# A four-stage sequence model on one core: stages issued by virtual time, and the scan's decay computed in place

## The chip, the cores and the metric

The kernel runs on one core of one Trainium2 chip. The metric is the device time in microseconds of one launch, and the time of before is the median of three runs. Besides these there is one execution under the hardware profiler; every duration below comes from it.

## The reference

The input is sixteen sequences of 512 tokens with 256 features, float32. Each sequence passes through four residual blocks, each fed with a layernorm of its input:

```
x = x + mamba(layernorm(x))        # selective scan, 16 states for each of 256 features
x = x + ffn(layernorm(x))          # 256 -> 704 -> 256, silu gate
x = x + attention(layernorm(x))    # causal linear attention, 16 heads of 16, elu + 1
x = x + ffn(layernorm(x))          # the same weights again
```

Inside, cut to what matters:

```
# mamba: u = x w_in; dt, B, C are projections of u
dt = softplus(dt_low @ w_dt + b_dt) * (DT_MAX - DT_MIN) + DT_MIN
h[d, n] = exp(dt[d] * A[d, n]) * h[d, n] + sum over d of (dt * A * B * u)
y[d] = sum over n of (h[d, n] * C[n]) + Dp[d] * u[d]
# ffn: activations and weights are quantised to FP4 in blocks of 16 and back
h = silu(xq @ wq_gate) * (xq @ wq_up);  out = quant(h) @ wq_down
# attention: num / den, with running sums of k v and of k over time
```

The time step of the recurrence is the token, so one sequence's scan is a chain along 512 tokens. The term that is added to the state is the same for all 256 features.

## The kernel before, in words

**One sequence, four stages.** Tokens lie 128 to a partition group (four chunks), or features on partitions and tokens along the row. The program writes the stages as generators that yield now and then, and a driver decides which generator goes on next. The order in which instructions are written is a priority: the Tile framework then places each engine's instructions at build time, by readiness and that priority, and each engine runs its list in order.

**Scan.** `front(b)` computes layernorm statistics and turns x into features (`tT_m`). `prologue(b)` computes dt (lines 456 to 471, through the tile `soft`), writes dt to DRAM as `dd` in eight DMAs from SP's queue (L476), computes u (L467), C (`cm`), and the state's input term `inp` (L485 to L496). `mamba(b)` then makes 16 steps. In each, `spread` reads a slice of `dd` back, repeated over 16 partitions, into one of three tiles `sp` (L509); `decay` makes two exponentials (L521) and a square (L524) on ACT into one of `NBAR = 2` tiles `bar`; DVE runs the recurrence over 2 x 512 elements (L540) and multiplies with C (L544); PE sums over the states into `py` (L550). At the end of each half, ACT copies `py` to `yT` (L555), and after the second half the output is turned back and added to x (L377).

**FFN.** Quantise x (L230 to L252), two matmuls for gate and up in halves of 352 columns (L592), tanh on ACT (L598), two products on DVE (L599, L600), quantise h, transpose (L614), down projection (L627). The first FFN (`_f` in tile names) has buffers of its own, and so has the second (`_g`).

**Attention.** q and k features (L664 to L672), a copy `ko` of k with the even heads zeroed (L681), then for each chunk scores (L710), the causal mask on DVE (L717), values (L741), a denominator spread by POOL (`dx`, L751), and the projection (L788).

**Shared resources.** All PSUM results but `py` take turns in seven banks. The tags `soft` (used for `soft`, `dtu` and `yT`), `dt` (used for `dt` and `inp`), `u`, `cm` and `tT` have one buffer each, so `soft` of sequence b + 1 can only be written once `yT` of sequence b has been read.

**The driver.** For each b, `first(b)` is scan b with `front(b + 1)` woven in, followed by the first FFN of b with `prologue(b + 1)` woven in. `by_turns` shares out each part: the scan goes beside `last_ffn(b - 2)`, and the first FFN with the prologue goes beside `attention(b - 1)`. While scan 0 runs, the FFN weights are quantised and transposed beside it.

Of the kernel before, what the change touches and what calls it, by code (L numbers as in the profile page):

```python
# [17 lines left out]
P = 128  # L18
# [14 lines left out]
def kernel(  # L33
# [31 lines left out]
    NBAR = 2  # L65
    NSP = 3
# [20 lines left out]
    xp = ctx.enter_context(tc.tile_pool(name="xp", bufs=4))  # L87
# [10 lines left out]
    begun, turned, stats = {}, {}, {}  # L98
# [59 lines left out]
    for t in vpads:  # L158
        nc.gpsimd.memset(t, 0.0)

# [283 lines left out]
    def prologue(b):  # L444

        xnT = turned.pop(b)
# [18 lines left out]
        u = one.tile([P, ND, S], F32, tag="u", name=f"u_{b}")  # L465
        for e in range(ND):
            nc.scalar.copy(u[:, e, :], from_xn(w_in_sb[:, :, ts(e, P)], f"pu{e}"))  # L467
        yield 0.5
# [11 lines left out]
        cm = one.tile([P, S], F32, tag="cm", name=f"cm_{b}")  # L480
        nc.scalar.copy(cm, from_xn(w_c_sb, "pcm"))


        dtu = one.tile([P, ND, S], F32, tag="soft", name=f"dtu_{b}")
        nc.vector.tensor_tensor(dtu, dt, u, ALU.mult)  # L485
        pg = bank(f"pg_{b}")
        for k in range(ND):
            nc.tensor.matmul(
                pg, a_rep[:, k].rearrange("p n i -> p (n i)"), dtu[:, k, :],
                start=(k == 0), stop=(k == ND - 1),  # L490
            )
        pb = from_xn(w_b_sb, "pbm")
        inp = one.tile([P, 2, S], F32, tag="dt", name=f"inp_{b}")
        nc.scalar.copy(inp[:, 0, :], pb)
        nc.vector.tensor_tensor(inp[:, 1, :], inp[:, 0, :], pg, ALU.mult)
        nc.scalar.copy(inp[:, 0, :], inp[:, 1, :])  # L496
        begun[b] = (u, dd, inp, cm)
        yield 2.5

    def mamba(b, xt):  # L500
        u, dd, inp, cm = begun.pop(b)

        yT = one.tile([P, ND, S], F32, tag="soft", name=f"yT_{b}")

        def spread(e, j, q0):

            sp = one.tile([P, 2, S], F32, tag="sp", name=f"sp_{b}_{e}_{j}_{q0}", bufs=NSP)
            src = dd[e, q0 // 2, j * G8 : (j + 1) * G8].rearrange("i q t -> i (q t)")
            nc.sync.dma_start(  # L509
                sp.rearrange("p q t -> p (q t)"),  # L510
                src.unsqueeze(0).to_broadcast([NS, G8, 2 * S]),
            )
            return sp

        def decay(sp, e, j, q0):

            bar = bars[state["bar"] % NBAR]
            state["bar"] += 1
            for i in range(2):
                g = 16 * e + 4 * (q0 + i) + j  # L520
                nc.scalar.activation(  # L521
                    bar[:, i, 1:S], sp[:, i, 1:S], AF.Exp, scale=a_col[:, g : g + 1]
                )
# [4 lines left out]
        sps = [spread(*steps[at]) for at in range(NSP - 1)]  # L528
        ahead = decay(sps[0], *steps[0])
        for at, (e, j, q0) in enumerate(steps):  # L530
            bar = ahead
            if at + NSP - 1 < len(steps):
                sps.append(spread(*steps[at + NSP - 1]))
            if at + 1 < len(steps):
                ahead = decay(sps[at + 1], *steps[at + 1])
            if j == 0 and q0 == 0:
                py = ps_y.tile([P, S], F32, tag="y", name=f"py_{b}_{e}")
                nc.tensor.matmul(py, d_diag[:, e], u[:, e, :], start=True, stop=False)
            h = one.tile([P, 2, S], F32, tag="hs", name=f"h_{b}_{e}_{j}_{q0}", bufs=3)
# [14 lines left out]
            if j == 3 and q0 == 2:  # L554
                nc.scalar.copy(yT[:, e, :], py)  # L555
# [15 lines left out]
    def ffn(i, nm, b, xt):  # L571
# [77 lines left out]
    def attention(b, xt):  # L649
# [29 lines left out]

        ko = att.tile([P, ND, S], F32, tag="ko", name=f"ko_{b}", bufs=1)  # L680
        nc.scalar.activation(ko, kf, AF.Copy, scale=odd_heads[:, 0:1])  # L681
        yield 0.1

        def scores(c):
# [19 lines left out]

            psc = [bank(f"psc_{b}_{c}_{g}") for g in range(4)]
            for s in range(NH // 4):
                e, odd = divmod(s, 2)
                for g in range(4):
                    rows = slice(32 * g, 32 * g + (2 * HD if odd else HD))
                    nc.tensor.matmul(  # L710
                        psc[g][:, ts(s, P)], (ko if odd else kf)[rows, e, tok],
# [15 lines left out]
        def attend(c, vp, sm):  # L727
# [22 lines left out]
            dx = att.tile([P, ND * HB, HD], F32, tag="dx", name=f"dx_{b}_{c}")  # L750
# [11 lines left out]
            if c < NC - 1:  # L762
# [3 lines left out]
                kt = att.tile([P, D], F32, tag="kt", name=f"kt_{b}_{c}")  # L766
# [71 lines left out]
    def first(b, scanned=False):  # L838
# [3 lines left out]
        more = b + 1 < B  # L842
        fr = front(b + 1, xs[b + 1]) if more else iter(())
        if not scanned:
            yield from weave(mamba(b, xs[b]), fr, 6)
        yield from fr
        yield from weave(ffn(0, "f", b, xs[b]), prologue(b + 1) if more else iter(()), 0)

    def last_ffn(b, i=1):
        yield from ffn(i, "g", b, xs[b])  # L850
        nc.sync.dma_start(out[b].rearrange("(c p) d -> p c d", p=P), xs[b])

    FIRST, CHUNKS, FRONT, ATTN, FFN2 = 76.0, 30.0, 4.15, 23.0, 40.0

    def some(gen, total):

        done = 0.0
        while done < total:  # L860
            piece = next(gen, None)
            if piece is None:
                return
            done += piece
            yield piece

    def by_turns(halves):

        done = [0.0] * len(halves)
        alive = list(range(len(halves)))  # L870
        while alive:
            i = min(alive, key=lambda i: done[i] / halves[i][1])
            try:
                done[i] += next(halves[i][0])
            except StopIteration:
                alive.remove(i)
# [56 lines left out]
```

## Time and profile before

| | |
|---|---|
| median of three runs | 2849.86 us (2844.62 to 2854.19) |
| profiled execution, its time | 2856.84 us |
| profiled execution, its span | 2855.1 us |
| mean granted TensorE clock | 0.929 |
| first scan step starts | 57.2 us |
| last scan step starts | 2568.8 us |

The span runs from the first instruction of the program to the last. PE is TensorE's matmuls, PEld its weight loads, DVE is VectorE, ACT ScalarE, POOL GpSimd, SP the engine from whose queue nearly all DMAs are issued. "L540" is line 540 of the kernel. Busy time of an engine is the union of its instructions' durations. Matmuls overlap in the pipeline and their ends are modelled, so a PE that is shown as busy is not necessarily full. In a group of instructions, the last part of a line gives the engine's idle time just before them and what ended it.

### The profile page before, as it was taken

What the parts mean: (1) busy time and instruction counts of PE and PEld (TensorE: products, weight loads), DVE (VectorE), ACT (ScalarE), POOL (GpSimd) and SP (SyncE); (2) the same over time, 40 slices, a digit from 0 to 9 for tenths busy, and PEclk for the clock granted to TensorE, in tenths of its full rate; (3) what the DMA queues carried; (4) which work ended last, traced back from release to release, by engine and by line L of the source; (5) the groups of instructions that cost most, each with busy time, mean ns of one, the idle gap of its engine ahead of it and who ended that gap; (6) DMA issues with size and microseconds to landing.
All of it is one profiled execution on the core that took longest, in us unless ns stands there. A gap on an engine that the chain in (4) does not pass through costs nothing.

```text
span 2855.1 us, 34186 instructions
## 1 busy us (share of the span) xinstructions
PE 2450.1 (86%) x12907; PEld 1451.0 (51%) x12907; DVE 2433.6 (85%) x3545; ACT 1493.4 (52%) x2798; POOL 154.6 (5%) x153
## 2 busy tenths in 40 slices
PE   6577989898988889898898989989898888988997
PEld 3143555454554545455554545545455454545664
DVE  7797888989798898979888898888979889897565
ACT  4666455555545555554555555555554555553322
POOL 2000000000000000000000000000000000000000
PEclk7788999999999999999999999999899999999988
DMA  5332104132230313213031320403222041320000
GB/s 146 89 96 74 52 1 106 36 82 60 56 73 13 102 39 82 60 38 89 15 96 45 82 60 9 110 23 85 56 59 74 8 103 38 74 59 7 2 1 15
DMA packets 64376, 165.26 MB, mean 58 GB/s; under 512 B 8434, under 2 KB 26836, under 8 KB 64212
## 3 DMA queue, kind: packets, MB, share of 16 engines
q1 hardware_dynamic: 62592, 162.03, 22.0%
q8 instruction: 101, 1.65, 0.2%
q10 hardware_dynamic: 1620, 1.06, 0.1%
q14 instruction: 63, 0.52, 0.1%
HBM read 146.28 MB, written 16.78 MB: 57 GB/s over the span
## 4 chain that ended last, share of the span: by engine, by line
DVE 45%; PE 38%; ACT 8%; issue 6%; POOL 2%; DMA 0%; SPq 0%; ACTq 0%; DVEq 0%; POOLq 0%
DVE h L540 15%; PE po_g L627 5%; DVE h L544 5%; PE pg_g L592 4%; PE pu_g L592 4%; PE pqk L664 3%; DVE sm L717 3%; PE po_f L627 3%; PE pu_f L592 2%; PE pg_f L592 2%; DVE amax_f L230 2%; PE py L550 2%; DVE v_f L244 2%; DVE h_f L600 2%; DVE x L377 1%
## 5 line engine op out<-in xcount | busy, mean ns | idle before, releaser
L540 DVE TENSOR_TENSOR_SCAN h<-bar,inp 128x1024 f32<-128x1024 f32 x256 | 581.6, 2281 | 31.8 <-ACT inp L496 22.4
L521 ACT ACTIVATE bar<-sp,a_col 128x511 f32<-128x511 f32 x512 | 348.6, 715 | 287.6 <-DVE h L540 278.9
L550 PE MATMUL py<-h,red 128*32 128x512 f32 x1024 | 284.7, 712 | 111.6 <-DVE h L544 111.6
L544 DVE TENSOR_TENSOR h<-h,cm 128x1024 f32<-128x1024 f32 x256 | 310.7, 1214 | 1.0
L524 ACT ACTIVATE bar<-bar 128x1022 f32<-128x1022 f32 x256 | 269.8, 1054 | 5.6
L627 PE MATMUL po_f<-wdT,hqT_f 128*128 128x256 f32 (+1 forms) x768 | 205.8, 412 | 24.8 <-ACT hqT_f L618 24.8
L627 PE MATMUL po_g<-wdT,hqT_g 128*128 128x256 f32 (+1 forms) x768 | 200.1, 403 | 31.4 <-ACT hqT_g L618 31.4
L627 PEld LDWEIGHTS po_f<-wdT,hqT_f 128*128 128x128 f32 (+1 forms) x768 | 142.7, 199 | 120.3 <-ACT hqT_f L618 61.3
L592 PE MATMUL pg_f<-wgT,tT_f 128*128 128x352 f32 x512 | 191.3, 498 | 12.8 <-DVE sm L717 9.5
L592 PE MATMUL pu_f<-wuT,tT_f 128*128 128x352 f32 x512 | 178.5, 472 | 18.7 <-DVE sm L717 18.4
L627 PEld LDWEIGHTS po_g<-wdT,hqT_g 128*128 128x128 f32 (+1 forms) x768 | 138.6, 193 | 92.0 <-ACT hqT_g L618 45.2
L592 PE MATMUL pg_g<-wgT,tT_g 128*128 128x352 f32 x512 | 178.3, 471 | 0.0
L592 PE MATMUL pu_g<-wuT,tT_g 128*128 128x352 f32 x512 | 173.2, 460 | 0.0
L717 DVE TENSOR_TENSOR sm<-psc,causal 128x512 f32<-128x512 f32 x256 | 162.9, 676 | 5.4 <-PE psc L710 4.1
L248 ACT ACTIVATE big_f<-v_f 128x704 bf16<-128x704 f32 (+1 forms) x80 | 67.4, 842 | 166.9 <-DVE v_f L244 166.3
L592 PEld LDWEIGHTS pu_f<-wuT,tT_f 128*128 128x128 f32 x512 | 99.2, 196 | 80.9 <-DVE sm L717 25.7
L550 PEld LDWEIGHTS py<-h,red 128*32 128x32 f32 x1024 | 35.7, 116 | 203.6 <-DVE h L544 171.1
L592 PEld LDWEIGHTS pg_g<-wgT,tT_g 128*128 128x128 f32 x512 | 94.9, 191 | 73.4 <-issue 33.4
L592 PEld LDWEIGHTS pg_f<-wgT,tT_f 128*128 128x128 f32 x512 | 92.8, 197 | 76.1 <-issue 17.7
L592 PEld LDWEIGHTS pu_g<-wuT,tT_g 128*128 128x128 f32 x512 | 97.8, 191 | 54.7 <-issue 1.0
L664 PE MATMUL pqk<-tT_a,w_qkv_sb 128*128 128x512 f32 x256 | 125.1, 617 | 0.0
L598 ACT ACTIVATE h_g<-pg_g 128x352 f32<-128x352 f32 x128 | 59.0, 461 | 95.6 <-PE pg_g L592 94.8
(235 smaller groups left out, 4614.7 us busy)
## 6 DMA issues: line engine op xcount, KB each, us to landing
sp<-dd SPq DMA_DIRECT2D x256, 512.0 KB, 4.7
x<-in_L_attn_a_x_dram SPq DMA_DIRECT2D x16, 512.0 KB, 5.0
dd<-dt SPq DMA_DIRECT2D x128, 64.0 KB, 1.7
out_dram<-x SPq DMA_DIRECT2D x16, 512.0 KB, 4.5
w_qkv_sb<-in_L_attn_b_W_attn_dram ACTq DMA_DIRECT2D x1, 768.0 KB, 7.2
raw_d<-in_L_ffn_w_down_dram SPq DMA_DIRECT2D x1, 704.0 KB
raw_g<-in_L_ffn_w_gate_dram SPq DMA_DIRECT2D x1, 640.0 KB, 7.2
raw_u<-in_L_ffn_w_up_dram SPq DMA_DIRECT2D x1, 640.0 KB, 6.5
```

Source lines behind the costliest of these rows:

```text
L230: nc.vector.tensor_reduce(amax, src.rearrange("p (b k) -> p b k", k=BLK), AX.X, ALU.max, apply_absolute_value=True,)
L248: nc.scalar.activation(big, v, AF.Abs, scale=STEP)
L521: nc.scalar.activation(bar[:, i, 1:S], sp[:, i, 1:S], AF.Exp, scale=a_col[:, g : g + 1])
L524: nc.scalar.activation(bar[:, :, 1:S], bar[:, :, 1:S], AF.Square)
L540: nc.vector.tensor_tensor_scan(h.rearrange("p i t -> p (i t)"), bar.rearrange("p i t -> p (i t)"), inp.rearrange("p i t -> p (i t)"), 0.0, ...
L544: nc.vector.tensor_tensor(h, h, cm.unsqueeze(1).to_broadcast([P, 2, S]), ALU.mult)
L550: nc.tensor.matmul(py[32 * q : 32 * q + 32, :], red[:, j, :], (h0, h)[q // 2][:, q % 2, :], start=False, stop=(j == 3),)
L592: nc.tensor.matmul(pw[:, :HF], xqT[:, k, ts(c, P)], wT[:, k, cols], start=(k == 0), stop=(k == ND - 1),)
L598: nc.scalar.activation(hc, pg[:, :HF], AF.Tanh, scale=0.5)
L627: nc.tensor.matmul(po[:, :D], hqT[:rows, r, :], wdT[:rows, r, :], start=(r == 0), stop=(r == NR - 1),)
L664: nc.tensor.matmul(pz, w_qkv_sb[:, k, ts(je, P)], xnT[:, k, :], start=(k == 0), stop=(k == ND - 1),)
L717: nc.vector.tensor_tensor(t, psc[g].rearrange("p (s t) -> p s t", t=P), causal.unsqueeze(1).to_broadcast([P, NH // 4, P]), ALU.mult,)
```

## The change

It concerns the order of work, and the way in which the scan gets its decay.

- **The driver.** `first`, `some`, `by_turns` and the nested halves go. Each stage of each sequence gets a start and a length in virtual time, and `run_all` always lets the stage that is furthest behind go on. Scan b fills period b; the first FFN takes 0.9 of the next one, attention 0.8 of the one after (from b + 1.95), the second FFN 0.9 from b + 2.8. Four sequences are under way.
- **The prologue moves.** `front` is now the first part of `prologue`, and `prologue(b + 1)` is woven into scan b, not into the first FFN of b. It holds dt first, and C; then it waits (`halfway`) until scan b has started its second half, since u of scan b is read until then, and computes u and the input term.
- **Buffers for it.** `inp` gets its own tag, and its two equal halves are filled at the start of the scan from `term`, one by ACT and one by POOL. `dt * u` is written over dt. `yT` is allocated when the first half ends. `cm` gets two buffers, `xp` five.
- **Decay in place of dt.** `sp` goes. The DMA brings dt straight to `bar`, 511 elements for each of two rows and starting at the second element, and the exponentials run in place. `NBAR` goes from 2 to 4, and a step's slice is asked for three steps ahead.
- **Attention.** `ko` is made chunk by chunk (128 x 256 each) instead of at once; `dx` and `kt` have one buffer instead of two.

```diff
-    NBAR = 2
-    NSP = 3
+    NBAR = 4
...
-    xp = ctx.enter_context(tc.tile_pool(name="xp", bufs=4))
+    xp = ctx.enter_context(tc.tile_pool(name="xp", bufs=5))
...
-    def prologue(b):
+    def prologue(b, xt):
 
+        yield from front(b, xt)
         xnT = turned.pop(b)
...
-        cm = one.tile([P, S], F32, tag="cm", name=f"cm_{b}")
+        cm = one.tile([P, S], F32, tag="cm", name=f"cm_{b}", bufs=2)
         nc.scalar.copy(cm, from_xn(w_c_sb, "pcm"))
-        dtu = one.tile([P, ND, S], F32, tag="soft", name=f"dtu_{b}")
-        nc.vector.tensor_tensor(dtu, dt, u, ALU.mult)
+        yield 0.1
+        while halfway[0] < b:
+            yield 0
+        u = one.tile([P, ND, S], F32, tag="u", name=f"u_{b}")
+        for e in range(ND):
+            nc.scalar.copy(u[:, e, :], from_xn(w_in_sb[:, :, ts(e, P)], f"pu{e}"))
+        yield 0.5
+        nc.vector.tensor_tensor(dt, dt, u, ALU.mult)
...
-        pb = from_xn(w_b_sb, "pbm")
-        inp = one.tile([P, 2, S], F32, tag="dt", name=f"inp_{b}")
-        nc.scalar.copy(inp[:, 0, :], pb)
-        nc.vector.tensor_tensor(inp[:, 1, :], inp[:, 0, :], pg, ALU.mult)
-        nc.scalar.copy(inp[:, 0, :], inp[:, 1, :])
+        term = dt[:, 0, :]
+        nc.scalar.copy(term, from_xn(w_b_sb, "pbm"))
+        nc.vector.tensor_tensor(term, term, pg, ALU.mult)
...
+        inp = one.tile([P, 2, S], F32, tag="inp", name=f"inp_{b}")
+        nc.scalar.copy(inp[:, 0, :], term)
+        nc.gpsimd.tensor_copy(inp[:, 1, :], term)
 
         def spread(e, j, q0):
-            sp = one.tile([P, 2, S], F32, tag="sp", name=f"sp_{b}_{e}_{j}_{q0}", bufs=NSP)
-            src = dd[e, q0 // 2, j * G8 : (j + 1) * G8].rearrange("i q t -> i (q t)")
-            nc.sync.dma_start(
-                sp.rearrange("p q t -> p (q t)"),
-                src.unsqueeze(0).to_broadcast([NS, G8, 2 * S]),
-            )
-            return sp
-        def decay(sp, e, j, q0):
             bar = bars[state["bar"] % NBAR]
             state["bar"] += 1
+            src = dd[e, q0 // 2, j * G8 : (j + 1) * G8, :, 1:S]
+            nc.sync.dma_start(bar[:, :, 1:S], src.unsqueeze(0).to_broadcast([NS, G8, 2, S - 1]))
+            return bar
+
+        def decay(bar, e, j, q0):
...
-                    bar[:, i, 1:S], sp[:, i, 1:S], AF.Exp, scale=a_col[:, g : g + 1]
+                    bar[:, i, 1:S], bar[:, i, 1:S], AF.Exp, scale=a_col[:, g : g + 1]
...
-        sps = [spread(*steps[at]) for at in range(NSP - 1)]
+        sps = [spread(*steps[at]) for at in range(NBAR - 1)]
...
-            if at + NSP - 1 < len(steps):
-                sps.append(spread(*steps[at + NSP - 1]))
             if at + 1 < len(steps):
                 ahead = decay(sps[at + 1], *steps[at + 1])
+            if at + NBAR - 1 < len(steps):
+                sps.append(spread(*steps[at + NBAR - 1]))
...
+    def scan(b):
+        if b + 1 < B:
+            xs.append(load(b + 1))
+            yield from weave(mamba(b, xs[b]), prologue(b + 1, xs[b + 1]), 1)
+        else:
+            yield from mamba(b, xs[b])
...
+    SCAN, FFN, ATTN = 65.7, 40.2, 25.7
+
+    def run_all(stages):
+        under_way = []
+        while stages or under_way:
+            if not under_way or (stages and stages[0][0] <= min(u[0] for u in under_way)):
+                begin, length, total, stage, *args = stages.pop(0)
+                under_way.append([begin, length / total, stage(*args)])
+                continue
+            now = min(under_way, key=lambda u: u[0])
+            try:
+                now[0] += next(now[2]) * now[1]
+            except StopIteration:
+                under_way.remove(now)
...
+    for b in range(B):
+        if b > 0:
+            stages.append((b, 1.0, SCAN, scan, b))
+        stages.append((b + 1.0, 0.9, FFN, ffn, 0, "f", b, xs))
+        stages.append((b + 1.95, 0.8, ATTN, attention, b, xs))
+        stages.append((b + 2.8, 0.9, FFN, last_ffn, b))
+    run_all(sorted(stages, key=lambda stage: stage[0]))
```

## The prediction, made before the change was run

> **What bounds the kernel now.** I read the page's busy shares first, then the span cut at the scan's own starts and ends (the view of windows), then DVE in order of time inside one of those stretches.
>
> ```profile
> PE 2450.1 (86%) x12907; PEld 1451.0 (51%) x12907; DVE 2433.6 (85%) x3545; ACT 1493.4 (52%) x2798; POOL 154.6 (5%) x153
> ```
>
> PE and DVE seem to be about equally busy, and neither is full. That is an average over two regimes. One sequence's scan runs from 778.0 to 882.4, the next starts at 945.3; the columns are busy time with instruction counts for PE, PEld, DVE, ACT, POOL, then granted clock, DMA share, GB/s:
>
> ```profile
> core 0: us, PE busy (x) PEld busy (x) DVE busy (x) ACT busy (x) POOL busy (x), PEclk, DMA share, GB/s
> 778.00:882.40 104.40, 86.43 (x584) 51.46 (x583) 101.45 (x138) 58.07 (x109) 8.04 (x7) 0.95 0.28 71
> 882.40:945.30 62.90, 59.72 (x221) 35.77 (x220) 47.99 (x83) 34.24 (x66) 1.01 (x1) 1.00 0.17 42
> ...
> 0.00:57.20 57.20, 36.16 (x111) 21.36 (x111) 39.59 (x69) 23.70 (x41) 17.04 (x27) 0.85 0.48 139
> ...
> 2571.00:2855.00 284.00, 242.40 (x1355) 160.94 (x1353) 183.72 (x326) 80.26 (x186) 7.10 (x12) 0.91 0.02 6
> ```
>
> While a scan runs, DVE is 97% busy (101.45 of 104.4) and PE 83%. Between two scans, PE is 95% busy (59.72 of 62.9) and DVE only 76%. So the period of 167.3 us holds 149.44 us of DVE work and 146.15 us of PE work, and the two engines are the bound in turn. DVE's idle time is 2.95 + 14.91 = 17.9 us per period, nearly all of it between the scans.
>
> Why is no scan work there to fill it? DVE in order of time at the end of that stretch (start, duration, engine, line, tiles; in brackets the idle time before and what ended it):
>
> ```profile
> 929.56 1.21 DVE L471 SCALAR_TENSOR_TENSOR dt<-soft,dt 128x1024 f32<-128x1024 f32 x1
> ...
> 943.04 0.69 DVE L495 TENSOR_TENSOR inp<-inp,pg 128x512 f32<-128x512 f32 x1 [5.31 <-ACT inp L494]
> 945.29 2.29 DVE L540 TENSOR_TENSOR_SCAN h<-bar,inp 128x1024 f32<-128x1024 f32 x1 [1.57 <-ACT inp L496]
> ```
>
> The next scan waits for its own prologue, which ends 62 us after the previous scan did. The prologue can't begin before yT is read (tag `soft`), and it is woven into the first FFN, so it stands in PE's saturated queue. The stretch is a serial link between scan b and scan b + 1.
>
> The groups that carry the scan and the edited parts:
>
> ```profile
> L540 DVE TENSOR_TENSOR_SCAN h<-bar,inp 128x1024 f32<-128x1024 f32 x256 | 581.6, 2281 | 31.8 <-ACT inp L496 22.4
> L521 ACT ACTIVATE bar<-sp,a_col 128x511 f32<-128x511 f32 x512 | 348.6, 715 | 287.6 <-DVE h L540 278.9
> ...
> L544 DVE TENSOR_TENSOR h<-h,cm 128x1024 f32<-128x1024 f32 x256 | 310.7, 1214 | 1.0
> ...
> sp<-dd SPq DMA_DIRECT2D x256, 512.0 KB, 4.7
> ```
>
> **The change part by part.**
>
> *Prologue under the scan.* This is the part that matters. It removes the link: when scan b ends, only `inp` of b + 1 has to be filled (one ACT copy of 0.61 us, the L496 row's mean, and a POOL copy), so scan work is always there for DVE. Its instructions are the same and move from the PE-bound stretch to beside the scan: per sequence 16 matmuls for statistics and transposition (1.95 us in a row), 28 of 512 columns and 16 ACT passes, 5.4 us of DVE, one x load (5.0 us to landing) and eight `dd` writes (1.7 us each). The writes now stand in SP's queue among the spreads; each issue takes about 0.45 us (8 took 3.63 us at 930.8), so a spread is held 3.6 us, of the lead worked out below. Its own chain, from the load to `term`, took 52 us (from the pt_m matmuls at 891 to 943) beside a full PE, and the `halfway` wait takes it to the scan's second half at the latest: some 75 us of a 154 us scan remain after it. I cost it at nothing; uncovered, each 10 us of lateness would be 10 us per period.
>
> *Order by virtual time.* DVE's and PE's totals do not change. If all four streams are mixed evenly, a period needs 149.44 / 0.97 = 154.1 us of DVE and 146.15 / 0.95 = 153.8 us of PE, each at the best share that it shows today. Both would have to be near their best at once. I take DVE at 95% instead, 157.3 us, 10 us less than 167.3.
>
> How hard PE presses is where a rule matters. The Trainium skill, Perfetto Trace Analysis, Identifying the Most-Contended Engine, says that matmul busy time misjudges a PE's load and that weight-load busy time (or MFU) should be used. By the PE row, PE would be at 93% (146.15 of 157.3) and two nearly full in-order engines would block each other; I'd put DVE no higher than 91%, a period of 164. By the rule it is (51.46 + 35.77) / 157.3 = 55%, and DVE alone counts, at 97%: 154. The trace is between: in the PE-bound stretch weight loads stand at 57% (35.77 of 62.9) with PE clearly saturated, so 55% is not much room; but there the matmuls lay under 0.95 of busy time for at least 63 us on end. That is why I take 95%, and keep both ends.
>
> *Decay in place, four bars.* The page's largest ACT wait, 278.9 us for `bar` behind the scan's read, goes: an exponential now waits only for its DMA. What waits is the spread on SP's queue, for the scan step three earlier; behind it are other spreads, `dd` writes, x loads and outputs. The lead is three steps of about 157 / 16 = 9.8 us, 29 us, against 4.7 us to landing. ACT was not the bound (52%), and while it waited DVE was 97% busy: gain 0 to 3% of the scan stretch, inside my 95%. The price is in the DMA: rows of 511 elements (2044 B) instead of 1024 (4096 B). Perfetto Trace Analysis, DMA Optimizations, speaks against it: transfers under 2 KB have a significant overhead each. The row is 4.7 us for 512 KB; no row has this shape. If the landing doubled to 9.4 us it would still be under 29, and DMA engines that are 28% busy would be at most 56% busy. So 0 by both; if the lead were gone, 16 x 4.7 = 75 us per sequence would be exposed.
>
> *POOL's half of `inp`.* ACT loses nothing (two copies before, two after); POOL gains 16 copies of 128 x 512. `dx`, 128 x 256, takes 0.55 us on average, so 1.1 us each, at the scan's start. GPSIMD Engine Reference, Key points, says that POOL shares its SBUF interfaces with VectorE when that reads two SBUF inputs, as the scan does: at worst 16 x 1.1 = 18 us. In the trace the scan step has a median of 2282 ns and a maximum of 2380, though 64 `dx` copies and 64 `rstd` steps of 1.0 to 1.9 us run on POOL meanwhile, so I take 0 and keep 18.
>
> *The rest.* `ko` in chunks: 4 passes of about 0.37 us (the 128 x 256 copies, e.g. L767) for one of 1.15, so 0.33 us more ACT per sequence, hidden at 52%. One buffer for `dx` and `kt`: chunk c + 1's waits for chunk c's transposes; chunks are about 30 us apart (a fifth of a period and more), so 0; if not covered, under 1 us a chunk, 64 us at most. `cm`, `xp`: only more room.
>
> **The sum.** The head to the first scan stays 57.2. The tail has the same content (the trace has the 14th sequence's second FFN and the 15th's attention after the last scan already): 284, of which I take 280, since the last sequence's FFN no longer starts late. Between them lie 2433.6 - 39.6 - 183.7 = 2210.3 us of DVE work, which took 2514 us (88%). At 95% it takes 2327. Sum 2664, 191 less than the span of 2855.1. The profiled execution's time was 2856.8, 7 above the median of 2849.9; I give 2660 for the median.
>
> **The rivals.**
>
> *A: the mix reaches only 91%.* Both engines nearly full, matmul results waiting in seven banks for a DVE that is busy with 2.28 us scan steps. 2210.3 / 0.91 = 2429, with 337 for the ends 2766, some 2762. For it: the PE row as weighed above. Against: during a scan DVE keeps 97% with three other streams about.
>
> *B, slower: banks.* Scores take four of the seven banks at once (`psc`) until DVE has masked them (0.68 us each, L717), and FFN halves take two each. Today half of this is evacuated by a DVE with 24% idle; with four streams each DVE consumer stands behind scan steps for the whole period, PE stops for want of banks, and DVE then for want of PE. It decides from the point where DVE's share of the middle falls under 2210.3 / (2855 - 337) = 88%; at 83%, which is a period of 180, the time is 2663 + 337 = 3000. For it: PE waits of this kind (`pu_f` behind `sm`, 25.7 us in all) exist. Against: they are small in a scan stretch that has the same mixture.
>
> *C: it doesn't do what it says.* The framework orders instructions by readiness, and the trace has the stages of four sequences beside each other already. If the list comes out much the same and the link merely moves, the time stays at 2840 to 2858.
>
> *D: both engines are better than I take.* 97% and a tail of 250: 2279 + 307 = 2586.
>
> **How the numbers follow.** The likeliest, 2600 to 2720, has 0.60; A (2720 to 2840) 0.16; D 0.04; C 0.03; B 0.17. About 0.3%, 9 us, is what a measurement of this kernel can tell from no change. So faster 0.80, same 0.03, slower 0.17. The range leaves out B, and D's lower end, and holds the rest with POOL's 18 us: 2580 to 2850.
>
> **What would show it right or wrong.** Right: scan starts some 157 us apart with no stretch between the last step of one and the first of the next; DVE at 93% or more in every period; the ACT wait for `bar` behind L540 gone; `inp` no longer waited for by several us; half-clock stretches fewer, clock above 0.93. Wrong: weight loads waiting for `sm` or `x` by hundreds of us (B), `bar` waiting for the spread's DMA or SP's queue, scan steps longer than 2.3 us beside POOL, the first step late after `term`, or a tail much above 284 us.

## The result and the profile after

The changed kernel takes 3004.32 us (median of four runs, 3003.07 to 3005.55) against 2847.6 for before (median of four, one run more than in the table above): a ratio of 1.0547, 95% interval [1.0526, 1.0568]. It is slower by 157 us where 190 less were forecast, and lies outside the range. The profiled execution has a span of 3001.4 us and a granted clock of 0.885 (before 0.929).

The busy shares on the page of after, to be held against the same line of before:

```profile
PE 2484.2 (83%) x12907; PEld 1528.3 (51%) x12907; DVE 2452.6 (82%) x3545; ACT 1485.8 (50%) x2846; POOL 184.9 (6%) x171
```

The instructions are the same in number on PE and DVE, and DVE's work has grown by 19 us only. What grew is idle time: DVE's from 421 to 549 us of the span, PE's from 405 to 517. The span of after cut into its head, one period between two first scan steps (1070 to 1248) with two stretches inside it, and the end from the last scan step on (columns as in the windows of before):

```profile
core 0: us, PE busy (x) PEld busy (x) DVE busy (x) ACT busy (x) POOL busy (x), PEclk, DMA share, GB/s
0.00:61.00 61.00, 33.90 (x103) 19.74 (x103) 43.47 (x90) 29.55 (x50) 18.71 (x31) 0.83 0.52 147
1070.00:1158.00 88.00, 69.01 (x305) 43.41 (x302) 78.45 (x113) 52.66 (x101) 8.23 (x5) 0.83 0.31 78
1158.00:1236.00 78.00, 70.96 (x436) 43.87 (x435) 60.00 (x96) 34.68 (x67) 1.48 (x3) 0.96 0.11 28
1070.00:1248.00 178.00, 151.45 (x801) 94.03 (x797) 150.41 (x219) 91.75 (x177) 10.91 (x9) 0.89 0.22 56
2636.00:3001.40 365.40, 298.05 (x1665) 201.89 (x1662) 221.95 (x396) 100.89 (x243) 9.64 (x15) 0.89 0.02 6
```

The scan does start directly after the scan. But the period is 178.0 us where before's was 167.3, and it holds the same work: DVE 150.41 us (84.5%), PE 151.45 (85%). The two regimes of before haven't gone: they have moved inside the period. In its first 88 us DVE is 89% busy (78.45) and PE 78%; in the next 78 us PE is 91% busy (70.96) and DVE 77%. The end is 365.4 us long and holds 221.95 us of DVE work, 38 more than the last 284 us of before.

What the first regime looks like, in DVE's order of time in that period:

```profile
1086.41 0.88 DVE L230 TENSOR_REDUCE amax_f<-h_f 128x44 f32<-128x704 f32 x1
...
1088.28 1.16 DVE L230 TENSOR_REDUCE amax_g<-xn_g 128x64 f32<-128x1024 f32 x1
...
1092.59 1.21 DVE L244 TENSOR_TENSOR v_g<-xn_g,inv_g 128x1024 f32<-128x1024 f32 x1
1093.72 0.88 DVE L251 SCALAR_TENSOR_TENSOR v_f<-big_f,v_f 128x704 f32<-128x704 bf16 x1
1094.52 0.16 DVE L389 TENSOR_SCALAR var_m<-mv_m 128x4 f32<-128x4 f32 x1
1094.59 2.28 DVE L541 TENSOR_TENSOR_SCAN h<-bar,inp 128x1024 f32<-128x1024 f32 x1
1096.79 0.86 DVE L252 TENSOR_TENSOR h_f<-v_f,half_f 128x704 f32<-128x704 f32 x1
```

Three stages want DVE together: the first FFN quantises h (`h_f`), the second FFN quantises its input (`xn_g`), and the scan runs. PE in the same stretch, and what it waits for (brackets):

```profile
1086.42 4.57 PE L631 MATMUL po_f<-wdT,hqT_f 128*128 128x256 f32 x12 [2.53 <-ACT hqT_f L622]
1090.92 1.98 PE L551 MATMUL py<-h,red 128*32 128x512 f32 x12
1097.71 1.36 PE L618 MATMUL pt_h_f<-ident,h_f 128*128 128x128 f32 x6 [4.81 <-DVE h_f L252]
```

PE's next instruction needs `h_f`, whose last pass stands behind the scan step and the other FFN's passes; PE is idle for 4.81 us. From 1158 on it is the other way round: PE has matmuls of both FFNs in a row, and DVE is short of work. Over the whole execution, the list of waits has for PE's weight loads, first before, then after:

```profile
PEld pt_h_f L614 <- DVE h_f L252: 7.2, 2, 3.6
```

```profile
PEld pt_h_f L618 <- DVE h_f L252: 93.3, 16, 7.3
```

A wait that came twice comes about once in every sequence. Kernels without it will turn out to be as slow, though. And the decay: two groups of after and its two largest ACT waits.

```profile
L541 DVE TENSOR_TENSOR_SCAN h<-bar,inp 128x1024 f32<-128x1024 f32 x256 | 578.5, 2277 | 24.0 <-PE py L551 13.7 <-ACT bar L523 6.4 <-POOL inp L506 2.6
bar<-dd SPq DMA_DIRECT2D x256, 511.0 KB, 4.7
```

```profile
ACT bar L520 <- DMA bar<-dd: 261.3, 141, 9.1
ACT h_g L602 <- PE pg_g L596: 212.8, 84, 11.8
```

The wait behind the scan's read (278.9 us) is gone and one of the same size for the DMA stands in its place. The other line, tanh waiting for the gate's matmuls, was 94.8 us in before. The scan step itself costs what it did (2277 ns, 2281 before), and it waits little for `bar` (6.4 us in all): what pays is what stands behind the exponential in ACT's list. The chain that ended last shows it, at the start of the same stretch (start, us, engine, tile):

```profile
1075.92 6.23 DMA bar<-dd
...
1082.80 0.71 ACT bar L520
...
1084.35 0.94 ACT bar L523
...
1085.90 0.48 ACT hqT_f L622
...
1086.42 4.58 PE po_f L631 x12
```

The copy `hqT_f`, on which the down projection waits, stands in ACT's list behind exponentials that wait for the DMA. Over the whole execution `bar<-dd` is 8% of this chain; in before DMA is 0% of it.

### The profile page after: what moved, and what is told of

Same layout as the page of the kernel before. It is cut to its first block, busy times and chain, and to the rows that moved or that the text cites. A ratio compares the mean times of both kernels' runs of the same rounds, so it can differ in the third digit from the quotient of the medians.

```text
span 3001.4 us, 34162 instructions
## 1 busy us (share of the span) xinstructions
PE 2484.2 (83%) x12907; PEld 1528.3 (51%) x12907; DVE 2452.6 (82%) x3545; ACT 1485.8 (50%) x2846; POOL 184.9 (6%) x171
## 3 DMA queue, kind: packets, MB, share of 16 engines
q1 hardware_dynamic: 95360, 161.77, 21.3%
## 4 chain that ended last, share of the span: by engine, by line
PE 37%; DVE 34%; ACT 12%; DMA 9%; issue 4%; POOL 3%; SPq 0%; DVEq 0%; POOLq 0%; ACTq 0%
DVE h L541 11%; DMA bar<-dd 8%; PE po_g L631 5%; PE pg_g L596 4%; PE pu_g L596 4%; PE po_f L631 3%; DVE h L545 3%; ACT bar L520 2%; PE pg_f L596 2%; PE pden L814 2%; PE pt_a L421 2%; PE pu_f L596 2%; ACT bar L523 2%; DVE v_f L250 2%; POOL rstd_a L391 1%
## 5 line engine op out<-in xcount | busy, mean ns | idle before, releaser
L541 DVE TENSOR_TENSOR_SCAN h<-bar,inp 128x1024 f32<-128x1024 f32 x256 | 578.5, 2277 | 24.0 <-PE py L551 13.7
L520 ACT ACTIVATE bar<-bar,a_col 128x511 f32<-128x511 f32 x512 | 353.1, 717 | 284.5 <-DMA bar<-dd 261.3
L551 PE MATMUL py<-h,red 128*32 128x512 f32 x1024 | 234.8, 665 | 62.4 <-DVE h L545 62.3
L631 PE MATMUL po_g<-wdT,hqT_g 128*128 128x256 f32 (+1 forms) x768 | 226.2, 443 | 71.5 <-ACT hqT_g L622 71.5
L631 PE MATMUL po_f<-wdT,hqT_f 128*128 128x256 f32 (+1 forms) x768 | 236.6, 459 | 42.0 <-ACT hqT_f L622 41.9
L631 PEld LDWEIGHTS po_f<-wdT,hqT_f 128*128 128x128 f32 (+1 forms) x768 | 161.8, 225 | 135.8 <-ACT hqT_f L622 72.7
L596 PE MATMUL pg_g<-wgT,tT_g 128*128 128x352 f32 x512 | 201.8, 516 | 1.1 <-DVE x L638 1.1
L603 DVE SCALAR_TENSOR_TENSOR h_g<-h_g,pg_g 128x352 f32<-128x352 f32 x128 | 66.2, 518 | 120.8 <-ACT h_g L602 120.7
L754 POOL COPY dx<-den 128x256 f32<-128x256 f32 x64 | 31.6, 494 | 1709.5 <-PE pr L759 1185.0
L618 PE MATMUL pt_h_f<-ident,h_f 128*128 128x128 f32 (+1 forms) x384 | 63.4, 309 | 77.7 <-DVE h_f L252 77.5
L713 PE MATMUL psc<-qk,ko 32*128 32x128 f32 x1024 | 81.7, 314 | 55.1 <-ACT ko L706 55.1
```

The lines of the kernel that those rows point to most:

```text
L520: nc.scalar.activation(bar[:, i, 1:S], bar[:, i, 1:S], AF.Exp, scale=a_col[:, g : g + 1])
L541: nc.vector.tensor_tensor_scan(h.rearrange("p i t -> p (i t)"), bar.rearrange("p i t -> p (i t)"), inp.rearrange("p i t -> p (i t)"), 0.0, ...
L551: nc.tensor.matmul(py[32 * q : 32 * q + 32, :], red[:, j, :], (h0, h)[q // 2][:, q % 2, :], start=False, stop=(j == 3),)
L596: nc.tensor.matmul(pw[:, :HF], xqT[:, k, ts(c, P)], wT[:, k, cols], start=(k == 0), stop=(k == ND - 1),)
L603: nc.vector.scalar_tensor_tensor(hc, hc, 1.0, pg[:, :HF], ALU.add, ALU.mult)
L618: nc.tensor.transpose(pt[:rows, ts(r - r0, P)], h[:, r * P : r * P + rows], ident)
```

## The experiments

Ratios are to runs of before on the same chip, with 95% intervals. "DVE" and "clock" are DVE's busy share and the granted clock from 800 to 2300 us of each profiled execution, in the view of windows.

| kernel | order | decay | ratio | DVE | clock |
|---|---|---|---|---|---|
| before | old | own tile | 1 | 0.882 | 0.95 |
| after | virtual | in place | 1.0547 [1.0526, 1.0568] | 0.838 | 0.90 |
| e1c_trim | virtual | in place | 1.0501 [1.0458, 1.0544] | 0.837 | 0.90 |
| e1_own_yT | virtual | in place | 1.0614 [1.0573, 1.0655] | 0.830 | 0.90 |
| e5_diag | virtual | in place | 1.0646 [1.0626, 1.0666] | 0.833 | 0.90 |
| e6_diag_yT | virtual | in place | 1.0685 [1.0668, 1.0703] | 0.832 | 0.90 |
| e7_sp_diag_yT | virtual | own tile | 1.0491 [1.0473, 1.0509] | 0.846 | 0.92 |
| e4_sp | virtual | own tile | 1.0730 [1.0709, 1.0751] | 0.816 | 0.89 |
| e3_old_driver | old, prologue in scan | in place | 1.1006 [1.0961, 1.1052] | 0.796 | 0.88 |
| e2_decay_only | old | in place | 1.0455 [1.0405, 1.0505] | 0.846 | 0.93 |
| e8_six_bars | old | in place | 1.0452 [1.0397, 1.0507] | 0.841 | 0.93 |
| e9_tied | old | in place, tied | 1.0290 [1.0268, 1.0313] | 0.870 | 0.95 |
| e10_first70 | old, shifted | own tile | 1.0347 [1.0296, 1.0397] | 0.849 | 0.92 |
| f6_first78 | old, shifted | own tile | 1.0072 [1.0048, 1.0097] | 0.879 | 0.94 |
| f2_small_shift | virtual, shifted | in place | 1.0920 [1.0904, 1.0936] | 0.819 | 0.89 |
| f1_stagger_only | staggered | in place | 1.0380 [1.0364, 1.0397] | 0.857 | 0.91 |
| f3_stagger_in_place | staggered | in place | 1.0267 [1.0234, 1.0300] | 0.866 | 0.93 |
| f5_stagger_tied | staggered | in place, tied | 1.0231 [1.0208, 1.0254] | 0.866 | 0.95 |
| e11_stagger | staggered | own tile | 0.9907 [0.9890, 0.9924] | 0.891 | 0.95 |
| f4_stagger_later | staggered, shifted | own tile | 1.0507 [1.0489, 1.0524] | 0.850 | 0.93 |

The time follows DVE's share through the table with small exceptions. That says that no kernel has more to do (DVE's busy time is 2426 to 2469 us in all of them) and that each fits the same work together better or worse; it doesn't say why. In the expectations the theories have numbers in the order in which they were formed: T1 is a buffer shared by two sequences, T2 that any mixture of four streams blocks itself, T3 the decay in place, T4 the shared tile `diag`, T5 starts that coincide, T6 that any shift places all lists anew.

**Is it a shared buffer?** After's scan has a hole in the middle of its period (no scan step from 1158.6 to 1208.2 us; DVE is 72% busy meanwhile), in which `yT` of scan b waits for the prologue's dt in the same buffer (`soft`) until 1173 us; after that the sums over the states stand behind other matmuls in PE's list until 1207. e1 gives `yT` its own tag and pays for it with single buffers in attention; e1c pays without getting.

```diff
-        yT = one.tile([P, ND, S], F32, tag="soft", name=f"yT_{b}")
+        yT = one.tile([P, ND, S], F32, tag="yT", name=f"yT_{b}")
...
-            yT = att.tile([P, ND, P], F32, tag="yTc", name=f"yT_{b}_{c}")
+            yT = att.tile([P, ND, P], F32, tag="yTc", name=f"yT_{b}_{c}", bufs=1)   # ko and num too; these alone in e1c
```

> The changed kernel with one edit, and room made for it: yT gets a tag of its own instead of sharing the one buffer of the tag soft; ko, num and yTc of attention go from two buffers to one to pay for its 4 KB. Theory T1 (the shared buffer): in the changed kernel the copy of the first half's result to yT waits for dt of the next sequence, whose prologue is late on PE; so py is not free, the second half's state sums wait, the three h buffers fill, and the scan stops for about 50 us in each period of 179 us. Without the sharing the hole goes, the period falls to 155 to 165 us and the time to 2650 to 2800. Theory T2 (the mixture itself, my rival B: banks and in-order queues block each other whatever the buffers): the period stays over 172 and the time at 2920 to 3010. Theory T3 (exponentials wait for the spread's DMA in ACT's queue): also 2950 to 3010, with ACT's wait for bar behind the DMA still at 260 us.

> The control for the run with its own yT: the changed kernel with only the three attention tiles at one buffer, yT still in the tag soft. All theories: 2990 to 3040, at most 1% over the changed kernel, since each chunk has some 30 us.

The payment costs nothing (1.0501 [1.0458, 1.0544], beside after's 1.0547). With the buffer the hole goes from the middle of the scan, but a stretch of 51 us without scan work opens at its end (the last step starts 129 us after the first, the next scan at 180), and the kernel is slower, 3033 us, above what any of the three theories had given. T1 fell. A hole needn't cost much either: e11, the fastest kernel below, has one of 45 us (841.6 to 886.2), in which DVE is 87% busy with other stages. The buffers of `diag`, also shared by all streams, were split next, alone (e5) and with `yT` (e6):

```diff
-        tag="diag", name=f"diag_{name}", bufs=1)
+        tag=f"diag_{name[0]}", name=f"diag_{name}", bufs=1)
```

> The changed kernel, with attention's small tiles as in the control, and one edit: the tile diag, which attention and the next prologue share in one buffer, gets one for each. Theory T4: the prologue's transposition can't start before attention's matmuls have read diag, and attention comes late, so the next scan's input comes late: with a diag of its own the prologue's matmuls move from 80 us into the period to under 50, and the period falls by 5 to 15 us, the time to 2780 to 2930. T3: within 1% of the control, 2970 to 3030, since ACT's DMA waits stay.

> The changed kernel with diag apart and yT apart (five instead of six masked score tiles pay for it). If only the two shared buffers kept the scan waiting (T1 and T4 together, each hiding the other), 2650 to 2780. T3: 2950 or more.

Neither helps (3032.51 and 3042.18 us; T4 fell). More room makes this order no better.

**Is it the decay in place?** e2 is before with this one part of the change, e8 the same with six tiles instead of four.

```diff
-                    bar[:, i, 1:S], sp[:, i, 1:S], AF.Exp, scale=a_col[:, g : g + 1]
+                    bar[:, i, 1:S], bar[:, i, 1:S], AF.Exp, scale=a_col[:, g : g + 1]
...
+    NBAR = 4    # 6 in e8
```

> The kernel before with one part of the change: decay in place of dt, four bars, the slice asked for three steps ahead; order, prologue and input term as before. T1 and T2: no harm from this part, 2830 to 2865; T3 (the decay's DMA is what costs): slower by as much as the whole change, 2930 or more.

> The kernel before with decay in place, as in the run with that part alone, but six bars and the slice asked for five steps ahead instead of three (num at one buffer to make room). Theory T3a: three steps are too short a lead when scan steps come in bursts 4 us apart, so the slice lands late; with five the wait for the DMA goes and the time returns to 2840 to 2880. T3b: ACT's list is written with the exponentials right behind the slice's expected landing, and the real landing is later however long the ring is; the wait for the DMA stays at 200 us or more and the time at 2940 to 3000. T6: any other placement of the instructions costs some per cent; then the time could be anything from 2850 to 3000, whatever the wait does.

The part that was costed at nothing takes 135 us by itself in the old order. The largest ACT wait of e2, then of e8:

```profile
ACT bar L516 <- DMA bar<-dd: 318.8, 169, 5.5
```

```profile
ACT bar L516 <- DMA bar<-dd: 246.5, 123, 4.8
```

An exponential stands at the head of ACT's list and waits 1.9 us (318.8 in 169 times) for a transfer that is still under way. Two more tiles shorten the waits by 72 us and the time not at all (2987.97 against 2987.12): the length of the ring is not it. In e9 the exponentials also wait for the scan step two before, so that they can't enter the list early; the wait for the DMA falls to 7.4 us, and one of 277.0 us for the tie takes its place.

```diff
+                gate = small.tile([P, 1], F32, tag="gate", name=f"gate_{b}_{e}_{j}_{q0}", bufs=2)
+                nc.gpsimd.tensor_scalar(gate, h[:, 0, 0:1], 0.0, None, ALU.mult)
...
-                    bar[:, i, 1:S], bar[:, i, 1:S], AF.Exp, scale=a_col[:, g : g + 1]
+                    bar[:, i, 1:S], bar[:, i, 1:S], AF.Exp, scale=a_col[:, g : g + 1], bias=gate
```

> The kernel before with decay in place and four bars, as in the run with that part alone, but each step's exponentials are tied to the scan two steps earlier, as they were in the kernel before: POOL makes a zero column from that step's result and the exponentials take it as their bias (256 POOL instructions of a column more; the values are unchanged). T3b: the exponentials then stand in ACT's list behind a DVE event, the slice has long landed, the wait for the DMA falls under 80 us and the time to 2840 to 2890. T3a: no change from the tie, 2950 or more. T6: 2850 to 3000.

The time falls by 46 us, about a third of the loss, where T3 in this form had said 2890 at most. The tie has a cost of its own: DVE is idle for 86.9 us before scan steps, 19.6 in e2. The other way round, the changed kernel with the old decay and its tiles `sp`:

```diff
-    NBAR = 4
+    NBAR = 2
+    NSP = 3     # 2 in e7, which also has the buffers of e6
```

> The changed kernel with the old decay: three tiles sp for the slices and two bars, the slice asked for two steps ahead; the stages by virtual time and the prologue under the scan stay; ko, num and yTc at one buffer to make room, as in the control. After the first runs, where decay in place alone cost 4.7% and yT's own buffer gained nothing, theory T3 says that the in-place decay is the loss: ACT's list then no longer stops for the slice's DMA (261 us of waits), and the time falls by some 130 to 160 us, to 2840 to 2880, the level of the kernel before. T2 (the mixture) says that the order is a loss of its own and the two do not add: 2950 or more. If T3 holds and my forecast for the order was right as well, it would be 2650 to 2750.

> The changed kernel with the old decay (two tiles sp, two bars), diag apart and yT apart: nothing of the change is left but the order and the place of the prologue, with no shared buffer between scan and prologue. If the causes are the in-place decay and the shared buffers, this is where my forecast should come true: 2620 to 2750. If the mixture itself is a loss (T2): 2850 or more.

e7 is 54 us faster than e6, which differs from it by the decay; e4 is 56 us slower than e1c, which differs from it by the decay as well. The sign isn't even constant, and T3, which had 2840 to 2880 for e4, fell as the whole cause.

**Is it the driver?** e3 is the changed kernel, prologue under the scan and all, issued by before's `by_turns`, its two shares set anew to the parts' new lengths (80.6 and 25.3).

> The changed kernel with the driver of before: the prologue stays under the scan, decay in place stays, yT stays in the tag soft, but the stages are taken in the two parts of before (scan beside the second FFN of two sequences earlier, then the first FFN beside attention). T1: the shared buffer is there, but in the scan's part PE is less full, so the prologue comes early enough for most of the hole to vanish: 2700 to 2880. T2: with less mixture than in the changed kernel 2800 to 2900, but not under the kernel before by over 1%, since the two regimes are back. T3: 2950 or more, since the decay is the same.

The slowest kernel of all, 3147.52 us. Virtual time is 4.6 points better for this body than the old driver with these shares. But how much is the driver, and how much the constants in it? e10 and f6 are before with two constants shifted and nothing else:

```diff
-    FIRST, CHUNKS, FRONT, ATTN, FFN2 = 76.0, 30.0, 4.15, 23.0, 40.0
+    FIRST, CHUNKS, FRONT, ATTN, FFN2 = 70.0, 36.0, 4.15, 23.0, 40.0    # e10; 78.0, 28.0 in f6
```

> The kernel before with one constant of its driver changed and nothing else: the share of first(b) that is written beside the second FFN is 70 instead of 76 units, the rest 36 instead of 30. T6 (the written order is tuned so closely that a small shift costs as much as the whole change): 2900 or more. Otherwise within 1.5% of before: 2810 to 2890.

> The kernel before with FIRST = 78 and CHUNKS = 28 in place of 76 and 30 and nothing else, a third of the shift that cost 3.5% and in the other direction. If the placement answers to any shift (T6) and before holds a favourable draw: slower by 1 to 4%. If before stands on a smooth optimum: within 1% of it.

Six units cost 3.5%, two cost 0.7%, with the instructions of before unchanged. The shift changes which generator writes next, hence the priorities, and the framework places the lists anew. The traces show it: of the pairs of DVE instructions that follow each other directly in before, 40% still do in e10 and 51% in f6 (after to e1c, whose times hardly differ, keeps all of them, and e2 to e8 95%). Before's constants are better than these two neighbours; f6 stayed within the 1% that a smooth optimum was given, so nothing shows that it is a narrow one.

**Do coinciding starts make the regimes?** In after, FFN, attention and second FFN start at b + 1, 1.95 and 2.8: within a fifth of a period of each other, seen from the scan. e11 is e7 with the three starts a third of a period apart.

```diff
-        stages.append((b + 1.0, 0.9, FFN, ffn, 0, "f", b, xs))
-        stages.append((b + 1.95, 0.8, ATTN, attention, b, xs))
-        stages.append((b + 2.8, 0.9, FFN, last_ffn, b))
+        stages.append((b + 1.0, 0.62, FFN, ffn, 0, "f", b, xs))
+        stages.append((b + 1.65, 0.62, ATTN, attention, b, xs))
+        stages.append((b + 2.3, 0.65, FFN, last_ffn, b))
```

> The run with the old decay, diag apart and yT apart (2988), with one edit in the driver's table: the three stages beside the scan get 0.62 to 0.65 of a period and start at b + 1.0, b + 1.65 and b + 2.3 instead of b + 1.0, b + 1.95 and b + 2.8, so that they no longer start within a fifth of a period of each other. Theory T5: their starts, which need DVE and little PE, coincide, and so do their later parts, which fill PE; the two regimes are rebuilt inside the period. Staggered, the period falls from 177 to 155 to 168 us and the time to 2650 to 2830. T2 in general (any mixture of four streams blocks): 2950 or more.

2830.74 us (2830.59 to 2832.89): 158 less than e7, and 0.9% faster than before. Its windows, a period and the stretch of the table:

```profile
794.00:961.00 167.00, 148.65 (x808) 88.16 (x808) 149.13 (x221) 93.20 (x177) 9.54 (x9) 0.97 0.24 60
```

```profile
800.00:2300.00 1500.00, 1338.89 (x7180) 794.27 (x7179) 1335.87 (x1968) 831.15 (x1580) 85.88 (x81) 0.95 0.24 60
```

A period of 167 us with DVE and PE both at 89%. And the wait that marked after is nearly gone from the list:

```profile
PEld pt_h_f L623 <- DVE h_f L253: 10.5, 16, 2.5
```

2831 us is at the edge of T5's range, and T2, which had 2950 or more, fell. But that wait isn't what decides: it is small in slow kernels too (28.0 us in e6, 21.3 in e7, 6.3 in f4). And one kernel proves little where a constant alone is worth 3.5%. So four more: f1 is after with these three lines only; f2 is after with two starts moved by 0.05 that stay together (1.9 and 2.75); f3 is e11 with the decay in place; f4 is e11 with all three starts 0.05 later.

> The changed kernel with three virtual times altered and nothing else: first FFN b+1.0 for 0.62, attention b+1.65 for 0.62, second FFN b+2.3 for 0.65. T5 (the three stages start within a fifth of a period, so their DVE-heavy and PE-light openings coincide, and this is what costs most): 2830 to 2890, DVE share of the middle 0.87 to 0.90, scan steps without a hole of over 40 us. T6 (the framework's list is only rerolled by any shift, and the staggered kernel with its other buffers was a lucky draw): anywhere from 2930 to 3060. If the decay in place has its own price in the staggered order, the time is above 2870 with an ACT wait for the DMA of over 150 us.

> The changed kernel with attention from b+1.9 in place of b+1.95 and the second FFN from b+2.75 in place of b+2.8; the three starts still lie within a quarter of a period. A gauge of how far a shift of 0.05 periods moves the time. T5: 2960 to 3050, two regimes inside the period as before. T6: it may fall anywhere, below 2900 too.

> The staggered kernel that took 2831 us, with the change's decay in place and four bars put back in place of the separate dt tile and two bars; all else equal. If the decay in place costs by itself in any order: 2880 to 2960. If its price in the old order was only a bad placement: 2815 to 2850.

> The staggered kernel with all three starts 0.05 periods later (b+1.05, b+1.7, b+2.35). T5: 2815 to 2880, since the starts stay apart. T6: the gain is lost, 2900 or more.

f1 gains 46 us on after. Its end is 76 us shorter (289.4 us from the last scan step on in place of 365.4) and its middle 29 longer, as 41 us of DVE's work have moved from one to the other; DVE's share of the middle rises from 85% to 86%, where T5 had 87 to 90.

```profile
2665.00:2954.40 289.40, 238.75 (x1376) 159.29 (x1368) 180.56 (x322) 83.14 (x201) 9.37 (x13) 0.91 0.02 6
```

f2 loses 108 us. And f4, the fast kernel moved by a twentieth of a period with its starts as far apart as ever, loses all of the gain and more: 2994.21. Its middle:

```profile
800.00:2300.00 1500.00, 1280.63 (x6836) 767.06 (x6829) 1274.56 (x1843) 776.87 (x1480) 82.94 (x77) 0.93 0.21 56
```

T5 fell as the deciding cause: starts apart are not enough. T6 stands, with one shift of 0.05 periods tried in each kind of order: 3.7 points from after to f2, 6.0 from e11 to f4. Of DVE's neighbouring pairs 34% and 36% are left. Which of the changed places costs the time, no run shows.

**Does the decay have a price of its own there?** f3 costs 92 us over e11. f5 puts e9's tie into f3.

> The staggered kernel with the decay in place (2923 us, 92 more than with the separate dt tile), and in it each pair of exponentials also waits for the scan two steps earlier, through a zero column that POOL derives from that scan's result and that serves as the exponentials' bias. If the price of the decay in place is that ACT's list has exponentials at its head whose DMA is still under way: the ACT wait for the DMA goes under 30 us and the time falls to 2830 to 2870. If the price is only another placement of all lists: the wait goes and the time stays within 40 us of 2923, or rises.

The wait for the DMA goes from 274.8 us to one case of 6.4, and an ACT wait for the gate takes its place:

```profile
ACT bar L525 <- POOL gate L521: 393.8, 147, 7.5
ACT bar L525 <- DMA bar<-dd: 6.4, 1, 6.4
```

The time stays (1.0231 [1.0208, 1.0254] against f3's 1.0267 [1.0234, 1.0300]). So in three of four pairs the decay in place costs 2 to 4.5 points, and in the fourth it gains 2.3. Taking the wait for the DMA away gave a third back in one order and nothing that can be told from zero in the other. That doesn't give the wait's price, since the tie itself makes DVE wait (80.6 us before scan steps in f5, 30.9 in f3) and both steps place the lists anew (38% of DVE's pairs are left from f3 to f5, 35% from e11 to f3). What can be said is that `bar<-dd` is 4 to 11% of the chain that ended last in all eleven kernels with the decay in place and no tie, and that DMA is at most 2% of it in all others. How much of the loss is the wait and how much the placement stays open.

## Why the prediction was wrong

By the terms of its own sum, 2664 = 57.2 + 2327 + 280, against the span of 3001.4:

- **Head.** 60.8 us to the first scan step; 4 us off.
- **Middle: the step that failed.** "I take DVE at 95% instead, 157.3 us." From the first scan step to the last (2636.3) it took 2575 us. DVE's work in it is 2452.6 - 43.5 - 222.0 = 2187 us, so the share is 85%; the miss is 248 us of the 337. The sum rested on "all four streams are mixed evenly", and virtual time didn't mix them: it only sets priorities, and in-order lists are placed by readiness, so that stretches of 89% and of 77% follow each other in one period. The scan stretch's 97% was read as what a mixture can do; before had a stretch of 76% after it, and no order that was tried has more than 89% from 800 to 2300 us. Neither reading of PE's load helped: matmul busy time had led to 91% for DVE, weight loads to 97%, and after has weight loads at 53% (94.03 of 178 us) with DVE at 84.5%. Why this order reaches 85% and e11's 89% is not known beyond the placement.
- **Tail.** 365.4 for 280, 85 us off. The prediction let the tail shrink by 4 us; with stages that start up to 2.8 periods behind their scan, more work is left when the last scan ends (222 us of DVE for 184), and it runs there at a share of 61%. f1's 289.4 and e11's 307.9, with starts up to 2.3 periods behind, point the same way; f4's 349.3, with 2.35, says that the placement counts here too.
- **Decay in place, "0 by both".** Right: the wait behind L540 goes, and the DMA with half the row takes 4.7 us as before. Wrong: the lead. Three steps of 9.8 us hold for an even scan; in after, steps of one scan start at 0, 4, 6, 25, 31, 36, 38 us and so on, so three steps can be some 6 us. It was put down as harmless since the scan would be spread, and what stands behind an exponential in ACT's list was not named: in after ACT waits 1.9 us for the DMA 141 times (261.3 us). The prediction had named "`bar` waiting for the spread's DMA" as a sign of being wrong, and it came. Alone in the old order the part cost 135 us (e2), new placement included.
- **Prologue under the scan.** Right in that the link went: scans start 178 to 181 us apart, directly one after the other. But the link was worth little: before's stretch of 62.9 us had been full on PE (95%), so what went with it was not idle time of the kernel but of DVE alone, and it came back elsewhere in the period. That "scan work is always there for DVE" did not come true: the hole of 50 us stands in the middle of nearly every period, and it begins with `yT` waiting for the prologue's late dt. Whether the prologue costs something where it now stands was not tried alone; the nearest pair is e3 and e2, both with the old driver and the decay in place, and e3, with the prologue under the scan and the rest of the change, is 160 us slower.
- **POOL's half of `inp`, `ko`, `dx`, `kt` at 0.** POOL's copies take 1.4 us on average (1.1 taken) and delay the scan by 2.6 us in all; the scan step has not grown. Right. `ko` in chunks was not free: in after the scores' weight loads wait for it once per sequence, 72.9 us in all, and in before they don't. No run took it alone, so its price isn't known.
- **Rival B.** Its size was right (83%, a period of 180, 3000 us), and that was luck, for its mechanism was not: the FFN's weight loads that waited for `sm` before (`pu_f` 25.7 us, `pg_f` 15.6) don't wait for it at all in after. Where PE waits for DVE, it is mostly for data (`h`, `h_f`, `run`) whose passes stand behind other work, not for a bank to come free.
- **What was missing.** No case said that the time depends this much on hand-set constants, so that a change which issues everything in another order may land far from what its idea is worth: there are 99 us between two sets of constants of before (e10), 108 between two of after (f2) and 163 between two of the staggered order (f4). The new order's constants were set once, and before's are better than the two that were tried beside them.

## What to carry to other kernels

A best share seen in one stretch is not what a mixture will reach: ask what paid for it in the next stretch. Where a framework places in-order lists from priorities, shift one of its constants by a little before believing any comparison of two orders: if the time moves by some per cent, one pair of kernels shows little about the idea, and the idea must be tried with several constants. A load into a tile that is then worked on in place can leave an instruction at the head of a list with only a DMA to wait for: count the lead in the shortest burst of its consumer, not in the mean, and look at what stands behind that instruction.

## What had not been expected

- A shift of a start by 0.05 periods, with the same instructions, took 2830.74 us to 2994.21 (e11 to f4), and 3004.32 to 3112.52 (after to f2). The runs of one kernel lie within 1.1% of each other, mostly within 0.5%.
- Inside after's period the granted clock was lower where PE was less busy: 0.83 where PE was 78% busy (1070 to 1158), 0.96 where it was 91% (1158 to 1236). The down projection of the second FFN takes 443 ns on average in after, 403 before. But it isn't the whole loss: e9 and f5 have before's 0.95 in the table and lose 2.9% and 2.3%, and PE's busy time per period rose by 5 us only (146 to 151).
- Rows of 2044 B in place of 4096 B, which are small by the Trainium skill (Perfetto Trace Analysis, DMA Optimizations, under 2 KB) if each row counts as a transfer, cost nothing in the landing: 4.7 us for 511 KB and for 512 KB, at a DMA share of 0.22 in the period.
